# Storing every slot in pairs, with 32 KB pieces, in a streaming residual kernel

## The chip, the cores and the metric

The kernel runs on one core of a Trainium2 chip. The metric is the device time of one execution in microseconds; lower is better. The time before is 323.47 us, the median of three runs (323.29 to 323.54).

## The reference

For each of 128 samples a subject's number picks one of eight 128 x 128 weight matrices, and the sample is replaced by itself plus its product with that matrix, all in float32:

```python
w = weights[subjects]                          # (128, 128, 128) from (8, 128, 128)
out = jnp.einsum('bct,bcd->bdt', x, w)         # x is (128, 128, 1024)
return x + out
```

A sample is 128 x 1024 float32 values, 512 KB. 64 MB are read and 64 MB are written.

## The kernel before

A *slot* is four samples (`H * G` = 2 x 2), 2 MB: each of the 128 partitions holds 16 KB of it. SBUF holds 12 slots side by side in `x_all`, and the 32 slots of the input (`NT` = 32) pass through them in turn.

**Loads** are issued by ACT on its DMA queue, one DMA of 512 KB for each sample (`load`, line 127), with the source in rows of 16 KB. From slot 12 on, ACT waits until the slot's earlier content has been stored (line 205).

**GpSimd** waits for a slot's loads and releases TensorE through `s_ready` (lines 209 to 214). Loads and stores of a slot count on one semaphore, `s_slot`, so the counts are worked out by `emptied`.

**TensorE and VectorE** run a loop over the slots, in halves of two samples. `multiply` (line 159) does four matmuls into PSUM; `add` (line 174) adds the product to the slot in place and raises `s_added`, twice for each slot; `place` (line 154) copies the next weights.

**Stores** are issued by SP on its own DMA queue (line 216). Before a store SP waits for `s_added`: slot i is stored when slot i + 4 is added (`BEHIND` = 4), and the last eight slots (`LAST` = 8) without this delay. The first 20 slots are stored one at a time; the last 12 in pairs (`PAIR` = 2), each pair one DMA of 4 MB whose source is written as two pieces of 16 KB for each partition (`o=n`). The last pair's store stands behind the loop (line 240). Line 62, in the helper `transfer`, is the line of all these DMAs in the profile.

The order of DMAs in each of the two queues is that of the loops; both queues are worked on by the same 16 DMA engines.

Of the kernel before, what the change touches and what calls it, by code (L numbers as in the profile page):

```python
# [30 lines left out]
G = 2  # L31
H = 2
# [3 lines left out]
SLOTS = 12  # L36

P_SLOTS = 2

BEHIND = 4  # L40
LAST = 8

PAIR = 2

DMA = 16

# [8 lines left out]
def transfer(nc, engine, out, in_):  # L55

    later, nc._always_lower_symbolic_ap = nc._always_lower_symbolic_ap, False
    ins, outs = engine.lower_ap_dma(in_), engine.lower_ap_dma(out)  # L60
    nc._always_lower_symbolic_ap = later
    return engine.add_instruction(
        mybir.InstDMACopy(
            name=nc.get_next_instruction_name(),
            engine=engine.engine,
            ins=ins,
            outs=outs,
            mode="Copy",
            cce_op=ALU.bypass,
            queue=QUEUES[engine.engine],  # L70
        )
    )


@with_exitstack
def kernel(
    ctx: ExitStack,
    tc: tile.TileContext,
    x: bass.AP,
    subjects: bass.AP,  # L80
    weights: bass.AP,
    out: bass.AP,
):
    nc = tc.nc
    B, C, T = x.shape
    S, _, D = weights.shape
    NT = B // (G * H)

    def sbuf(name, *shape, dtype=F32):
        return ctx.enter_context(nc.sbuf_tensor(name, list(shape), dtype)).ap()  # L90


    room = -(nc.sbuf_base + -nc.sbuf_base % 32) % ALIGN
    if room:
        sbuf("room", C, room // 4)
    x_all = sbuf("x_all", C, SLOTS * H * G * T)
    xs = [
        x_all[:, i * H * G * T : (i + 1) * H * G * T].rearrange("c (q t) -> c q t", t=T)
        for i in range(SLOTS)
    ]  # L100
    w_all = sbuf("w_all", C, S, D)
    ws = [sbuf(f"w{i}", C, 1, D) for i in range(H * G)]
    zeros = sbuf("zeros", C, N)
    given, near, wrap = (sbuf(name, 1, B, dtype=I32) for name in ("given", "near", "wrap"))
    index = sbuf("index", 1, B + H * G, dtype=I32)
    ps = [
        ctx.enter_context(nc.psum_tensor(f"ps{i}", [D, G, T], F32)).ap() for i in range(P_SLOTS)
    ]

    s_given = tc.alloc_semaphore("s_given")  # L110
    s_wall = tc.alloc_semaphore("s_wall")
    s_index = tc.alloc_semaphore("s_index")
    s_zeros = tc.alloc_semaphore("s_zeros")
    s_product = tc.alloc_semaphore("s_product")
    s_added = tc.alloc_semaphore("s_added")

    s_ready = tc.alloc_semaphore("s_ready")
    s_go = tc.alloc_semaphore("s_go")

    s_slot = [tc.alloc_semaphore(f"s_slot{k}") for k in range(SLOTS)]  # L120
    s_head = tc.alloc_semaphore("s_head")

    def emptied(i):
        turns = i // SLOTS
        return DMA * (H * G + 1) * turns - (DMA * G if i >= SLOTS and i % SLOTS == 0 else 0)

    def load(engine, i, q):
        transfer(
            nc,
            engine,  # L130
            xs[i % SLOTS][:, q, :],
            x[i * H * G + q].rearrange("(a r) t -> a (r t)", r=ROWS),
        ).then_inc(s_head if i * H * G + q < G else s_slot[i % SLOTS], DMA)

    def store(i, n):
        at = i % SLOTS * H * G * T
        return transfer(
            nc,
            nc.sync,
            out[i * H * G : (i + n) * H * G].rearrange("g d t -> d g t"),  # L140
            x_all[:, at : at + n * H * G * T].rearrange("d (o t) -> d o t", o=n),
        )

    def subjects_of(i):
        _, subject = nc.values_load_multi_w_load_instructions(
            index[0:1, i] if isinstance(i, slice) else index[0:1, bass.ds(i * (H * G), H * G)],
            engines=[mybir.EngineType.DVE],
            min_val=0,
            max_val=S - 1,
            skip_runtime_bounds_check_because="the index is clamped on the chip above",  # L150
        )
        return subject

    def place(h, subject):
        for q in range(h * G, (h + 1) * G):
            copy = nc.vector.tensor_copy(ws[q], w_all[:, bass.ds(subject[q], 1), :])  # L156
        copy.then_inc(s_go, 1)

    def multiply(slot, h):
        nc.tensor.wait_ge(s_go, 1).then_inc(s_go, -1)  # L160
        nc.tensor.wait_ge(s_ready, 1).then_inc(s_ready, -1)  # L161
        for q in range(h * G, (h + 1) * G):
            for t in range(0, T, N):
                at = slot * (H * G * T) + (q * T + t)
                mm = nc.tensor.matmul(  # L165
                    ps[h][:, q % G, t : t + N],
                    ws[q][:, 0, :],
                    x_all[:, bass.ds(at, N)],
                    start=True,
                    stop=True,  # L170
                )
        mm.then_inc(s_product, 1)

    def add(slot, h):
        mine = x_all[:, bass.ds(slot * (H * G * T) + h * G * T, G * T)]
        nc.vector.wait_ge(s_product, 1).then_inc(s_product, -1)  # L176
        nc.vector.tensor_tensor(  # L177
            mine, ps[h].rearrange("d g t -> d (g t)"), mine, ALU.add
        ).then_inc(s_added, 1)

    with tc.tile_critical():  # L181

        nc.sync.dma_start(given, subjects.rearrange("(o b) -> o b", o=1)).then_inc(s_given, DMA)
        nc.sync.dma_start(w_all, weights.rearrange("s c d -> c s d")).then_inc(s_wall, DMA)

        nc.vector.memset(zeros, 0.0).then_inc(s_zeros, 1)  # L186
        nc.tensor.wait_ge(s_zeros, 1)
        for _ in range(IDLE):
            nc.tensor.matmul(  # L189
                ps[P_SLOTS - 1][:, G - 1, :N], zeros[:, :D], zeros, start=True, stop=True  # L190
            )

        nc.vector.memset(index[:, B:], 0).then_inc(s_index, 1)  # L196
        nc.vector.wait_ge(s_given, DMA)
        nc.vector.tensor_scalar(near, given, -S, S - 1, ALU.max, ALU.min).then_inc(s_index, 1)  # L198
        nc.vector.wait_ge(s_index, 2)
        nc.vector.tensor_scalar(wrap, near, 0, S, ALU.is_lt, ALU.mult).then_inc(s_index, 1)  # L200
        nc.vector.wait_ge(s_index, 3)
        nc.vector.tensor_tensor(index[:, :B], near, wrap, ALU.add).then_inc(s_index, 1)  # L202
        for i in range(NT):
            if i >= SLOTS:
                nc.scalar.wait_ge(s_slot[i % SLOTS], emptied(i))
            for q in range(H * G):
                load(nc.scalar, i, q)

        for i in range(NT):
            if i == 0:  # L210
                nc.gpsimd.wait_ge(s_head, DMA * G).then_inc(s_ready, 1)
                nc.gpsimd.wait_ge(s_slot[0], DMA * G).then_inc(s_ready, 1)
            else:
                nc.gpsimd.wait_ge(s_slot[i % SLOTS], emptied(i) + DMA * H * G).then_inc(s_ready, H)

        for i in [*range(NT - SLOTS), *range(NT - SLOTS, NT, PAIR)]:
            n = 1 if i < NT - SLOTS else PAIR
            nc.sync.wait_ge(s_added, (i + n + (BEHIND if i < NT - LAST else 0)) * H)
            if i + n < NT:
                store(i, n).then_inc(s_slot[i % SLOTS], DMA)  # L220


        nc.vector.wait_ge(s_index, 4)
        nc.vector.wait_ge(s_wall, DMA)
        subject = subjects_of(slice(0, H * G))
        for h in range(H):
            place(h, subject)
        with nc.vector.Fori(0, NT) as turn:  # L228
            subject = subjects_of(turn + 1)
            for h in range(H):  # L230
                add(turn % SLOTS, h)
                place(h, subject)
        with nc.tensor.Fori(0, NT) as turn:
            for h in range(H):
                multiply(turn % SLOTS, h)

    with tc.tile_critical() as waits:
        for i in range(NT - SLOTS, NT - PAIR, PAIR):
            nc.scalar.wait_ge(s_slot[i % SLOTS], emptied(i + SLOTS))
    last = store(NT - PAIR, PAIR)  # L240

    tc.add_manual_dep(
        last.ins,
        waits.name,
        mybir.DependencyInfo(mybir.DependencyClass.NoSync, mybir.DependencyReason.SCHED_ONLY),
        reason="the end of the program waits for it",
    )
# [27 lines left out]
```

## Time and profile before

| What | Value |
|---|---|
| Median of 3 runs | 323.47 us |
| The profiled execution | 323.24 us |
| Its span | 321.5 us |
| TensorE busy (matmuls) | 249.8 us, 78% |
| VectorE busy | 165.7 us, 52% |
| Bytes moved by the DMA engines | 134.76 MB, 419 GB/s over the span |
| Mean granted TensorE clock | 0.905 |

The span is the profiled stretch; the execution's own time is 1.74 us longer. In the rows of DMA queues, q10 is ACT's queue (the loads) and q1 is SP's (the stores, the weights and the subjects' numbers); after the name stand the packets, the megabytes, and the time that the packets took as a share of the 16 engines' time in the window. A row of a timeline has the start and the duration in us, then engine, line, operation, operands and count, and in brackets the engine's idle time just before, with what ended it. The rows of digits show a span or window in 40 equal slices, each digit the busy share in tenths.

### The profile page before, as it was taken

The numbers are of one execution on the slowest core, as the hardware profiler recorded it, in microseconds if no ns is written. First come the engines' busy times: TensorE is split into PE (matmuls) and PEld (weight loads), VectorE is DVE, ScalarE is ACT, GpSimd is POOL, SyncE is SP. The second block draws the span as 40 slices with busy tenths as digits, with TensorE's granted clock in tenths as the row PEclk, the third lists the DMA queues.
The fourth block names the chain that finished last, engine by engine and source line by source line (L and its number), as shares of the span: only waits on it lengthen the run. The fifth ranks groups of instructions, "written<-read, shape, count | busy, mean of one in ns | idle before, by whom it ended". The sixth has DMA issues, their size and how long they took to land. (4 is left out here: it accounts for less than half of the span.)

```text
span 321.5 us, 2368 instructions
## 1 busy us (share of the span) xinstructions
PE 249.8 (78%) x518; PEld 102.8 (32%) x518; DVE 165.7 (52%) x202; POOL 0.2 (0%) x4
## 2 busy tenths in 40 slices
PE   6999999999979666866888469999769995885000
PEld 2444444444433322322333124433323332331000
DVE  2377667767773366146365361776445766066000
POOL 0000000000000000000000000000000000000000
PEclk9999999999997799779999896999978999599555
DMA  7999999999999999999999999999999999999997
GB/s 283 428 424 424 426 424 391 428 426 426 428 432 428 423 430 424 426 424 424 426 426 428 430 430 426 426 426 428 424 424 424 420 426 430 426 428 424 430 424 318
DMA packets 11700, 134.76 MB, mean 419 GB/s; under 512 B 2482, under 2 KB 3507, under 8 KB 3507
## 3 DMA queue, kind: packets, MB, share of 16 engines
q10 hardware_dynamic: 6144, 67.12, 49.7%
q1 hardware_dynamic: 5554, 67.64, 49.7%
q14 instruction: 2, 0.01, 0.0%
HBM read 67.63 MB, written 67.11 MB: 419 GB/s over the span
## 5 line engine op out<-in xcount | busy, mean ns | idle before, releaser
L165 PE MATMUL ps<-x_all,w 128*128 x512 | 244.4, 635 | 42.2 <-PEq L161 27.6
L177 DVE TENSOR_TENSOR x_all<-ps,x_all 128x2048 f32 x64 | 146.6, 2291 | 124.9 <-DVEq L176 124.9
L165 PEld LDWEIGHTS ps<-x_all,w 128*128 128x128 f32 x512 | 101.0, 203 | 186.3 <-issue 185.8
L156 DVE COPY w<-w_all 128x128 f32 x132 | 23.1, 218 | 4.1 <-DMA w_all<-in_L_cond_weights_dram 4.1
L189 PE MATMUL ps<-zeros 128*128 128x512 f32 x6 | 5.5, 1088 | 1.7 <-DVE zeros L186 1.7
L189 PEld LDWEIGHTS ps<-zeros 128*128 128x128 f32 x6 | 1.8, 328 | 3.7 <-issue 2.1
L186 DVE MEMSET zeros<- 128x512 f32 x1 | 0.5, 485 | 1.0 <-SPq L181 1.0
L198 DVE TENSOR_SCALAR near<-given 1x128 int32<-1x128 int32 x1 | 0.2, 214 | 0.7 <-DMA given<-in_itok_B_dram 0.7
L202 DVE CUSTOM_DVE_ANT_0 index<-near,wrap 1x256 uint16<-1x256 uint16 x1 | 0.3, 280 | 0.0
L200 DVE TENSOR_SCALAR wrap<-near 1x128 int32<-1x128 int32 x1 | 0.2, 216 | 0.0
L262 POOL MEMSET const-bfloat16-1.0<- 128x1 bf16 x1 | 0.1, 101 | 0.0
L262 POOL MEMSET const-uint8-127<- 128x1 uint8 x1 | 0.1, 101 | 0.0
L262 POOL MEMSET const-float32-0.0<- 128x1 f32 x1 | 0.1, 98 | 0.2 <-issue 0.2
L262 POOL MEMSET const-float32-1.0<- 128x1 f32 x1 | 0.1, 98 | 0.0
L262 DVE BASE_LOAD x1 | 0.0, 21 | 0.1
L196 DVE MEMSET index<- 1x4 int32 x1 | 0.1, 62 | 0.0
## 6 DMA issues: line engine op xcount, KB each, us to landing
x_all<-in_x_dram ACTq DMA_DIRECT2D x128, 512.0 KB, 34.9
out_dram<-x_all SPq DMA_DIRECT2D x20, 2048.0 KB, 15.6
out_dram<-x_all SPq DMA_DIRECT2D x6, 4096.0 KB, 28.6
w_all<-in_L_cond_weights_dram SPq DMA_DIRECT2D x1, 512.0 KB, 5.0
given<-in_itok_B_dram SPq DMA_DIRECT2D x1, 0.5 KB
```

What stands on the lines that cost most here:

```text
L156: copy = nc.vector.tensor_copy(ws[q], w_all[:, bass.ds(subject[q], 1), :])
L165: mm = nc.tensor.matmul(ps[h][:, q % G, t : t + N], ws[q][:, 0, :], x_all[:, bass.ds(at, N)], start=True, stop=True,)
L177: nc.vector.tensor_tensor(mine, ps[h].rearrange("d g t -> d (g t)"), mine, ALU.add).then_inc(s_added, 1)
L186: nc.vector.memset(zeros, 0.0).then_inc(s_zeros, 1)
L189: nc.tensor.matmul(ps[P_SLOTS - 1][:, G - 1, :N], zeros[:, :D], zeros, start=True, stop=True)
L196: nc.vector.memset(index[:, B:], 0).then_inc(s_index, 1)
L198: nc.vector.tensor_scalar(near, given, -S, S - 1, ALU.max, ALU.min).then_inc(s_index, 1)
L200: nc.vector.tensor_scalar(wrap, near, 0, S, ALU.is_lt, ALU.mult).then_inc(s_index, 1)
L202: nc.vector.tensor_tensor(index[:, :B], near, wrap, ALU.add).then_inc(s_index, 1)
L262: nc = _bacc.Bacc("TRN2", target_bir_lowering=False, num_devices=1)
```

## The change

All 32 slots are stored in pairs. A pair's source is one piece of 32 KB for each partition (`o=1`); its destination is the same eight samples as for a pair before. SP issues the store of the pair (i, i + 1) when slot i + 4, the third behind the pair, is added (`BEHIND` = 3); the last eight slots wait for their own adds alone, as before. Stores have six semaphores of their own, `s_store`, one for each pair of slots in SBUF; ACT waits for one of them before it loads into the first slot of a pair, and `s_slot` counts loads alone. The compute on TensorE and VectorE is unchanged.

```diff
-BEHIND = 4
+PAIR = 2
+
+BEHIND = 3
 LAST = 8
-
-PAIR = 2
...
-    def emptied(i):
-        turns = i // SLOTS
-        return DMA * (H * G + 1) * turns - (DMA * G if i >= SLOTS and i % SLOTS == 0 else 0)
+    s_store = [tc.alloc_semaphore(f"s_store{k}") for k in range(SLOTS // PAIR)]
+
+    def stored(i):
+        return s_store[i % SLOTS // PAIR], DMA * (i // SLOTS + 1)
+
+    def loaded(i):
+        return s_slot[i % SLOTS], DMA * H * G * (i // SLOTS + 1) - (DMA * G if i % SLOTS == 0 else 0)
...
-    def store(i, n):
+    def store(i):
         at = i % SLOTS * H * G * T
         return transfer(
             nc,
             nc.sync,
-            out[i * H * G : (i + n) * H * G].rearrange("g d t -> d g t"),
-            x_all[:, at : at + n * H * G * T].rearrange("d (o t) -> d o t", o=n),
+            out[i * H * G : (i + PAIR) * H * G].rearrange("g d t -> d g t"),
+            x_all[:, at : at + PAIR * H * G * T].rearrange("d (o t) -> d o t", o=1),
         )
...
         for i in range(NT):
-            if i >= SLOTS:
-                nc.scalar.wait_ge(s_slot[i % SLOTS], emptied(i))
+            if i >= SLOTS and i % PAIR == 0:
+                nc.scalar.wait_ge(*stored(i - SLOTS))
             for q in range(H * G):
                 load(nc.scalar, i, q)
...
-        for i in [*range(NT - SLOTS), *range(NT - SLOTS, NT, PAIR)]:
-            n = 1 if i < NT - SLOTS else PAIR
-            nc.sync.wait_ge(s_added, (i + n + (BEHIND if i < NT - LAST else 0)) * H)
-            if i + n < NT:
-                store(i, n).then_inc(s_slot[i % SLOTS], DMA)
+        for i in range(0, NT, PAIR):
+            nc.sync.wait_ge(s_added, (i + PAIR + (BEHIND if i < NT - LAST else 0)) * H)
+            if i + PAIR < NT:
+                store(i).then_inc(stored(i)[0], DMA)
...
-    last = store(NT - PAIR, PAIR)
+    last = store(NT - PAIR)
```

6 lines of the change are left out of this document (3 added, 3 removed).

## The prediction

> **What bounds the kernel now.** I read the page first: the slices of the span, the DMA queues, the DMA issues.
>
> ```profile
> span 321.5 us, 2368 instructions
> DMA  7999999999999999999999999999999999999997
> q10 hardware_dynamic: 6144, 67.12, 49.7%
> q1 hardware_dynamic: 5554, 67.64, 49.7%
> out_dram<-x_all SPq DMA_DIRECT2D x20, 2048.0 KB, 15.6
> out_dram<-x_all SPq DMA_DIRECT2D x6, 4096.0 KB, 28.6
> ```
>
> The sixteen DMA engines are 90% busy or more in every slice but the first and the last, and the two queues fill 99.4% of them: ACT's loads (q10) and SP's stores (q1). So only two things move the time: the DMA engines' own work, and gaps in it. The packet counts tell the pieces. A load of 512 KB in pieces of 16 KB is 32 packets and 16 small ones that raise the semaphore; 128 x 48 = 6144. A 2 MB store is 128 + 16 and a 4 MB store 256 + 16; 20 x 144 + 6 x 272, with 1042 for the weights and the index, is 5554. So every piece is one packet of 16 KB now.
>
> Then the DMA view in three windows: late (stores alone), early (weights in pieces of 512 B), and with both queues full.
>
> ```profile
> DMA packets 493, 7.67 MB, mean 426 GB/s; under 512 B 25, under 2 KB 25, under 8 KB 25
> q1 hardware_dynamic: 1041, 0.52, 38.6%
> q1 hardware_dynamic: 662, 9.80, 57.7%
> q10 hardware_dynamic: 668, 7.28, 43.0%
> ```
>
> First line, 300 to 318 us: 468 large packets in 16 x 18 us of engine time are 615 ns each, and 426 GB/s makes a slot (2.097 MB) 4.92 us. Second, 1.5 to 6 us: 38.6% of 16 x 4.5 us over 1041 packets is 26.8 ns for 512 B. The last two, 60 to 100 us, matter most: the queues moved the same number of packets, 662 and 668, but not the same bytes. The engines take turns by packet, whatever its size, and a load's little semaphore packets use up turns too. An engine serves a slot's store in 8 turns and one small one; in those 9 turns the loads get 6 large packets and 3 small ones, three quarters of a slot, and it all takes 14 x 0.615 = 8.6 us.
>
> Last, the end: the DMA view from 285 to 286, from 286 to the end and from 319 to the end, and the timelines of PE, DVE and SP.
>
> ```profile
> q10 hardware_dynamic: 6, 0.00, 0.3%
> DMA packets 936, 14.29 MB, mean 402 GB/s; under 512 B 64, under 2 KB 64, under 8 KB 64
> q1 hardware_dynamic: 936, 14.29, 94.7%
> DMA  0699690600000000000000000000000000000000
> 274.85 10.14 PE L165 MATMUL ps<-x_all,w 128*128 x16 [5.21 <-PEq L161]
> 286.53 7.13 PE L165 MATMUL ps<-x_all,w 128*128 x16 [1.54 <-PEq L161]
> 285.23 2.29 DVE L177 TENSOR_TENSOR x_all<-ps,x_all 128x2048 f32 x1 [0.81 <-DVEq L176]
> 293.90 2.29 DVE L177 TENSOR_TENSOR x_all<-ps,x_all 128x2048 f32 x1 [0.81 <-DVEq L176]
> 256.99 40.38 SPq L62 DMA_DIRECT2D out_dram<-x_all  x5
> ```
>
> The first line holds the last packets of the loads, semaphores alone: the last slot lands within this microsecond, I take 285.7. From PE's start to its second add's end the last slot takes 296.19 - 286.53 = 9.66 us, the one before, with a PE that came out of 5.2 us of idling, 287.52 - 274.85 = 12.67. The last store is issued at the end of SP's row, 297.37 less its issue of about 0.6. At 286 the engines still hold 14.29 MB of stores, 10.10 of them not of the last pair: 23.7 us of work that covers the 10.8 us from there to the last store's issue, with 13 to spare. **This reserve is what lets the last slot's work cost nothing.** The last bytes leave at about 319.5, 2.0 us before the span ends.
>
> **The change part by part.** *Fewer packets.* 16 stores x 128 pieces of 32 KB replace 4096 of 16 KB: 128 fewer per engine. The straight line through 26.8 ns at 512 B and 615 ns at 16 KB has 7.8 ns per packet beside its bytes: 1.0 us less work, and 32 KB in 1.222 us. No row shows a 32 KB packet; I keep 2 us of gain and 1 us of loss as ends. Ten fewer DMAs' semaphores are ten small packets per engine, 0.1 us at most.
>
> *Waits.* ACT waits for stores 10 times instead of 20 and GpSimd's counts change; PE's and DVE's instructions stay. SP's wait now holds a pair until its third follower is added, i + 5 slots for the pair (i, i + 1), which is the count that let slot i go before; the first store starts when it did. Behind SP's wait stand only later stores. ACT gets two slots back at once. Does the load queue run dry in the middle? When a pair goes, loads up to slot i + 11 are out and about i + 6.2 are in (below), so some five slots of loads are queued, and a pair's store lets less than two through. Nothing for the middle: the queue of loads covers it.
>
> *Turns.* A pair's store is still 8 turns and a small one per engine, but each moves 32 KB. Against 6 loads' packets it takes 8 x 1.222 + 6 x 0.615 = 13.5 us, and in this time loads move three quarters of a slot, as they did during **one** slot's store. A pair now moves 2.7 times as much as the loads beside it, instead of 1.33 times for a slot. As the rate per pair (four slot moves) is 19.7 us, the store queue empties in every turn, and stores follow the adds as closely as the waits let them. The bytes are the same; the order of them is not: the reserve of stores at the end goes.
>
> *The end, step by step.* How far loads lead the adds:
>
> ```profile
> q10 hardware_dynamic: 520, 5.57, 45.5%
> q10 hardware_dynamic: 144, 1.57, 107.1%
> 46.40 0.66 SPq L62 DMA_DIRECT2D out_dram<-x_all  x1
> x_all<-in_x_dram ACTq DMA_DIRECT2D x7, 512.0 KB, 8.0
> DMA  0000009994000099940003899999999999998433
> ```
>
> From 257 to 286 us (first line) 5.57 MB of loads are left, 2.7 slots, when 28 slots are added: the lead is 1.3. It is the 12 us or so of a slot's compute at the mean pace of 9.85 us a slot, so I keep 1.2 for after. The second and third: a store issued at 46.40 has no packet until 50.4; with loads in front it takes 4 us to start. The last two (1.5 to 6 us): into idle engines the first packets run some 1.3 us after ACT's first issue at 0.9.
>
> When slot 26 is added (27 slots), stores up to 21 are done and 28.2 slots loaded; the pairs 22 and 24 go together, pair 26 one slot later. 3.8 slots of loads are left. In the 4 us to the start, 0.8 of them pass; during three pairs, 3 x 13.5 = 40.5 us, 2.25 more. Slot 29 lands some 18 us into them and is added 12 us on, so pair 28 stands behind them without a gap. The 0.75 slot that is left takes all its 13.5 us. So the last load lands as the last store but one ends, and nothing is left to cover the last slot's work.
>
> The sum, against the profiled execution: all but the last pair's bytes were out at 319.5 - 9.85 = 309.65, less 1.0 for the packets: 308.65. Then 0.8 from landing to PE's start, 11.2 of compute (between 9.66 and 12.67), 0.6 for SP's issue, 1.3 to the first packet, 9.85 for 4.19 MB, 2.0 to the end: 334.4 us of span. The gap is 13.9 us. The profiled execution took 323.24, 1.74 more than its span, and the median of the runs is 0.23 higher: 336.4. A lead that is 0.3 slot larger brings the last load 5 us earlier and the time to 331. I take 335. The ends of compute, start and packets reach from 333 to 341 for this case.
>
> **The rivals.** *A smaller gap.* If loads lead by two slots at the 27th add, 3.0 are left: 0.8 and 2.2 pass by the end of pair 26, two slots' moves before 308.65 and so near 299, and pair 28 alone (9.85 us) then covers part of the last slot. PE starts near 300.8, the last store's first packet comes at 314 in place of 308.65: 5.3 us of gap, 327.8. For it: two loads that land together are added one after the other; against it, the 1.3 measured. It reaches from 326 to 331.
>
> *The reserve holds: faster.* If at the last load's landing over 14 us of stores other than the last pair, some 6 MB, are still queued, no gap opens and the fewer packets stay as the whole effect: 323.47 - 1.1 = 322.4. That takes loads finishing 14 us before the stores' end, which means that an engine evens out bytes, not packets. The 9.80 MB against 7.28 at equal counts speak against it.
>
> *The change doesn't do what it says: no change.* If a piece of 32 KB is cut into packets of 16 KB or less, turns and packets stay as they are; pairs still give loads three quarters of a slot per slot stored, the reserve survives, and 323.4 results. For it: the trace has no packet above 16 KB. Against it: pairs were written as two pieces of 16 KB each, and the count of 272 shows one packet for each piece as the instruction names it. [...]
>
> **How the numbers follow.** Gap of some 14 us, 333 to 341 and down to 331 with the larger lead: 0.58. Smaller gap, 326 to 331: 0.24. Reserve holds: 0.10. Pieces cut: 0.08. The first two are slower, 0.82 in all; the third faster by 0.3%, 0.10; the fourth within 0.2% (0.65 us, about what a measurement of this kernel can tell from no change), 0.08. The range, 326 to 341, takes in the first two and leaves 0.18 out. Likeliest: 335.
>
> **What would show it.** Packets on the stores' queue: 16 x 144 + 1042 = 3346; 5394 or more would mean cut pieces. With both queues full, equal packet counts but over twice the bytes on q1; equal bytes there would sink the forecast. A last load's landing at 300 to 309 in place of 285.7, and then a hole of 5 to 15 us in the DMA row, with DVE's last add inside it and the last store's 9.85 us alone behind it. If the last add ends with stores other than the last pair still running, the forecast is wrong, and the time is near 322. If holes stand in the middle, the loads starve and my cover for the middle was wrong.

## The result, and the profile after

The changed kernel takes 341.7 us (median of 6 runs, 339.75 to 344.56), the kernel before 323.33 us on the same chip: a ratio of 1.0584, with a 95% interval of 1.0551 to 1.0616. The forecast was slower at 335 us, within 326 to 341. The direction came, and the mechanism in the main; the size is 6.7 us off and 0.7 us beyond the range. Times are medians of all runs, while the ratios go by means without the runs that are over 1.5% above the fastest of their kernel and, in the experiments, without the profiled one, so a ratio can differ a little from the quotient of two medians. The profiled execution took 341.22 us, 1.82 more than its span.

From the page of the changed kernel:

```profile
span 339.4 us, 2358 instructions
DMA  7999999999999999999999999999999999997047
GB/s 286 427 427 429 425 423 423 419 419 419 417 411 405 428 411 415 436 423 427 411 427 434 444 402 425 419 407 423 429 405 431 409 432 431 431 431 326 0 185 309
q10 hardware_dynamic: 6144, 67.12, 47.7%
q1 hardware_dynamic: 3346, 67.63, 47.1%
```

The row of DMA digits has a 0 in it, and the GB/s below it fall to 0: all 16 engines stand still near the end. The stores' queue has 3346 packets, the number that whole pieces of 32 KB give. The shares of both queues are 47.7% + 47.1% of 339.4, 321.7 us for each engine; before they were 319.6. So of 17.9 us of span, 2.1 are busier engines and 15.8 are engines without work.

The turns, in the DMA view from 275 to 285 us:

```profile
q1 hardware_dynamic: 108, 3.15, 73.7%
q10 hardware_dynamic: 105, 1.05, 24.9%
```

Nearly equal packets, three times the bytes on the stores' queue. 3.15 MB are 96 packets of 32 KB; 73.7% of 16 x 10 us over 96 is 1.228 us for one.

Then the end: the DMA view from 313.5 to 328 us, the view of windows, and the timelines of PE, DVE and SP:

```profile
DMA  2000000000000000000000000000000000000000
q1 hardware_dynamic: 6, 0.03, 0.5%
q10 hardware_dynamic: 1, 0.00, 0.0%
314.00:328.00 14.00, 9.36 (x16) 3.78 (x16) 5.12 (x6) 0.00 (x0) 0.82 0.00 0
314.47 9.36 PE L169 MATMUL ps<-x_all,w 128*128 x16 [8.43 <-PEq L165]
324.07 2.29 DVE L181 TENSOR_TENSOR x_all<-ps,x_all 128x2048 f32 x1 [0.81 <-DVEq L180]
289.16 38.32 SPq L62 DMA_DIRECT2D out_dram<-x_all  x2
```

The last load lands just before 313.9 us (one small packet of q10 is left in the window, and the digits stop after the first). From 314 to 328 us the DMA share, the last but one column, is 0.00, while PE and DVE do the last slot. Its second add ends at 326.36, SP issues the last store at 326.94 (the row's end, 327.48, less an issue of 0.54), and those 4.19 MB run alone. Before, 14.29 MB of stores stood behind the last load; now the last pair alone does.

How the loads ended, in the DMA view from 295, 300, 305 and 310 us (5, 5, 5 and 4 us long):

```profile
q10 hardware_dynamic: 43, 0.44, 21.0%
q10 hardware_dynamic: 35, 0.34, 16.5%
q10 hardware_dynamic: 15, 0.15, 7.0%
q10 hardware_dynamic: 5, 0.02, 1.0%
```

They don't stop, they fade. At 300 us 0.51 MB are left; at the 0.105 MB/us of 275 to 285 us that is 4.9 us of work, but it lasts almost 14. The engines don't end together: those that are done with their loads go on with stores alone (95.1% of the engines' time from 305 to 310 us), and the slot waits for the slowest engine (PE starts at 314.47 us, the last load lands just before 313.9). The trace doesn't name a packet's engine, but with the engines full 99% of the packets (the kernel before from 240 to 300 us, the changed one from 260 to 295 us) start within 4 ns of the end of an earlier packet, which is taken for the one before on the same engine. Followed in this way, the 16 engines end their last loads from about 295 to 312 us here, and from 283 to 285 us in the kernel before.

### The profile page after: what moved, and what is told of

Read it like the earlier page. It is cut to its first block, busy times and chain, and to the rows that moved or that the text cites. A ratio compares the mean times of both kernels' runs of the same rounds, so it can differ in the third digit from the quotient of the medians.

```text
span 339.4 us, 2358 instructions
## 1 busy us (share of the span) xinstructions
PE 254.1 (75%) x518; PEld 105.0 (31%) x518; DVE 165.7 (49%) x202; POOL 0.2 (0%) x4
## 2 busy tenths in 40 slices
DMA packets 9491, 134.76 MB, mean 397 GB/s; under 512 B 2321, under 2 KB 3346, under 8 KB 3346
## 3 DMA queue, kind: packets, MB, share of 16 engines
q10 hardware_dynamic: 6144, 67.12, 47.7%
q1 hardware_dynamic: 3346, 67.63, 47.1%
## 5 line engine op out<-in xcount | busy, mean ns | idle before, releaser
L169 PE MATMUL ps<-x_all,w 128*128 x512 | 249.6, 647 | 68.1 <-PEq L165 66.2
L169 PEld LDWEIGHTS ps<-x_all,w 128*128 128x128 f32 x512 | 103.3, 207 | 214.4 <-issue 213.7
L193 PE MATMUL ps<-zeros 128*128 128x512 f32 x6 | 4.5, 903 | 1.7 <-DVE zeros L190 1.7
```

Source lines behind the costliest of these rows:

```text
L169: mm = nc.tensor.matmul(ps[h][:, q % G, t : t + N], ws[q][:, 0, :], x_all[:, bass.ds(at, N)], start=True, stop=True,)
L193: nc.tensor.matmul(ps[P_SLOTS - 1][:, G - 1, :N], zeros[:, :D], zeros, start=True, stop=True)
```

## The experiments

Three readings stood against each other. *Turns*: a 32 KB packet gets one turn like a 16 KB packet, so stores outrun the loads and nothing is left to cover the last slot. *Waits*: pairing, the third follower and slots given back two at a time open the hole. *Long pieces*: packets above 16 KB move worse by themselves.

**Pieces of 16 KB, everything else as changed.**

```diff
-            x_all[:, at : at + PAIR * H * G * T].rearrange("d (o t) -> d o t", o=1),
+            x_all[:, at : at + PAIR * H * G * T].rearrange("d (o t) -> d o t", o=PAIR),
```

> All slots are still stored in pairs with the new waits and semaphores, but a pair's source is two pieces of 16 KB again. Turns: a store's turn is no longer than a load's, so stores don't outrun the loads; the last load lands near 295 us instead of 313.7, stores are still queued when the last add ends, the hole of some 15 us goes, and the time is 323 to 325 us. Waits (pairing, the third follower, slots given back two at a time open the hole): the hole stays and the time stays at 340 us or more. Slow pieces (32 KB pieces move slower by themselves): no hole either, 323 us.

Measured: 323.91 us, 1.0024 of before (1.0014 to 1.0034). Its page, and its DMA view from 296 us on:

```profile
span 322.7 us, 2358 instructions
DMA  7999999999999999999999999999999999999996
q1 hardware_dynamic: 662, 10.06, 88.6%
```

No load packet is left after 296 us, and 10.06 MB of stores still are: the reserve is back. The pairing, the waits and the semaphores cost 0.7 us; 17.7 of the 18.4 us need the long piece.

**Long pieces for the last 12 slots alone**, in the kernel before:

```diff
-            x_all[:, at : at + n * H * G * T].rearrange("d (o t) -> d o t", o=n),
+            x_all[:, at : at + n * H * G * T].rearrange("d (o t) -> d o t", o=1),
```

> The kernel before with one edit: its six pairs, the last 12 slots, are stored from one piece of 32 KB for each partition. The first 20 slots, all waits and all semaphores are those of before. Turns: only the order of transfers in the last 80 us decides whether the last slot is covered, so a hole before the last store comes back, 4 to 15 us long, and the time is 327 to 338 us. Waits: nothing of the new waits is there, 323.3 us. Slow pieces: 12 of 32 slots, so three eighths of the 18 us, about 330 us, but spread over the last third and without a hole.

Measured: 329.14 us (four runs, 328.42 to 334.28), 1.0183 (1.0154 to 1.0212). The page and the windows view:

```profile
span 326.6 us, 2368 instructions
DMA  7999999999999999999999999999999999999847
310.00:315.00 5.00, 1.06 (x3) 0.19 (x1) 3.06 (x6) 0.00 (x0) 0.85 0.00 0
```

A hole of at least 5 us, without one of the new waits; and with all of them, but pieces of 16 KB, there was none. As the cause of the hole *waits* is out. The order at the end makes the hole, but 12 slots of it make a third of the loss only.

**Late pairs held.** The pairs from slot 20 on, whose slots are not loaded again, wait for 27 adds at least (`HOLD` = 27), so the pairs 20, 22 and 24 go together; pieces of 32 KB stay.

```diff
-            nc.sync.wait_ge(s_added, (i + PAIR + (BEHIND if i < NT - LAST else 0)) * H)
+            nc.sync.wait_ge(s_added, (i + PAIR + BEHIND if i < NT - SLOTS else max(i + PAIR, HOLD)) * H)
```

> The changed kernel, 32 KB pieces and all, but the pairs from slot 20 on, whose slots are never loaded again, are held until 27 slots are added. Turns: loads run alone for longer before these stores begin, the last load lands before 290 us, four pairs or more stand queued at the last add, no hole, and the time is 322.4 to 325 us, with what the long pieces themselves cost or save as the rest. Waits: more holding is no cure, 341 us or more. Slow pieces: the 18 us stay, without a hole.

Measured: 329.05 us, 1.0156 (1.0117 to 1.0195). The hole is gone, as turns have it; 4 us more are left than the upper end that I gave. **The same with pieces of 16 KB** (`o=PAIR`):

> The kernel with the late pairs held until 27 slots are added, which took 329.0 us without a hole, with pieces of 16 KB instead of 32 KB. If the 5.8 us that were left there are the price of long pieces in the stretch where loads and stores share the engines (engines that stall and end apart from each other), they go and the time is 323 to 324 us. If the hold cost them, the time stays at 328 us or more.

In this run and in the one with pieces of 4 KB, the load of the subjects' numbers (0.5 KB, at the start) was split as well, into two and eight pieces.

Measured: 324.12 us, 1.0022 (1.0012 to 1.0031). So the long pieces have a second price of some 5 us that is no hole before the last store. The pages of both, 32 KB first:

```profile
span 328.7 us, 2358 instructions
GB/s 283 433 425 421 435 423 421 407 433 423 429 397 435 389 422 399 425 429 427 429 405 423 435 421 435 419 405 423 397 427 429 429 409 437 439 427 419 439 427 80
span 323.0 us, 2358 instructions
GB/s 282 424 426 422 424 424 390 434 428 426 422 428 424 427 430 430 422 422 426 426 426 420 432 422 424 424 420 430 422 428 424 424 424 430 432 424 426 424 428 264
```

With 32 KB the rate dips below 410 GB/s again and again in the middle, and the last slice, where engines end apart, moves 80 GB/s. The DMA view of the run with 32 KB from 320 us to its end:

```profile
DMA  3997073090033700330300300000300000000000
q1 hardware_dynamic: 45, 0.95, 25.7%
```

At 426 GB/s 0.95 MB are 2.2 us of work, but packets still start near 326 us. So the better part of the second price in this kernel is engines that end apart.

**Where the second price arises.** Long pieces for the first 20 slots alone, and, in the held kernel, for the held pairs alone:

```diff
-            x_all[:, at : at + PAIR * H * G * T].rearrange("d (o t) -> d o t", o=1),
+            x_all[:, at : at + PAIR * H * G * T].rearrange("d (o t) -> d o t", o=PAIR if i >= NT - SLOTS else 1),
...
+            x_all[:, at : at + PAIR * H * G * T].rearrange("d (o t) -> d o t", o=1 if i >= NT - SLOTS else PAIR),
```

> The changed kernel with 32 KB pieces for the first 20 slots alone; the last six pairs are stored in pieces of 16 KB. Turns: near the end loads and stores share as before, so there is no hole, or one under 3 us. What is left is the price of long pieces in the stretch where the store queue empties and fills again and again (held pairs in 32 KB pieces took 329.0 us, in 16 KB pieces 324.1): 325 to 329 us, with engines that end apart. If the order at the end were all, and long pieces in the middle cost nothing: 323.5 to 324.2 us.

> The held kernel (late pairs wait until 27 slots are added) with 16 KB pieces for the first 20 slots and 32 KB pieces for the held pairs, whose queue doesn't empty between them. If the price of long pieces comes with the emptying and refilling of the store queue: 323 to 324.5 us, no hole. If it comes with any 32 KB packets beside loads: 326 us or more.

Measured: 327.37 us (four runs, 326.91 to 330.72), 1.016 (1.0104 to 1.0217), and 324.02 us, 1.0025 (1.0015 to 1.0034). So the price comes with the first 20 slots, where the stores' queue empties and fills again (in the changed kernel three times, for some 17 us each). Held pairs, whose queue stays full, cost nothing that shows; but only 309 of their 768 long packets ran beside loads, against 1280 for the first 20 slots. A price for every such packet would make 0.8 to 1.0 us there, and the kernel stood as near to the one before as its like with pieces of 16 KB. This favours the emptying and doesn't prove it.

The trace of the changed kernel tells a little more. From 60 to 260 us, half of the loads' packets take 616 ns or less, as before, but 98 of 2496 take over 700 ns, against 11 of 2530 before. Of these 98, 55 ran at 124 to 128 and at 244 to 248 us, where stores begin again after some 17 us of loads alone. Why they take longer, no run tells.

The losses don't add: 4.1 us for the middle, 5.9 for the end, 18.4 for both. With long pieces at the end alone, the engines' last loads end within 2 us of each other, in the changed kernel within some 18; so engines that the middle has driven apart seem to make the uncovered end longer. No run tests this by itself.

**Loads in pieces of 8 KB, stores in pieces of 16 KB:** the ratio of sizes is two again, with nothing above 16 KB (`ROWS = 2`, `o=PAIR`).

> All pairs in pieces of 16 KB, which by itself took 323.9 us without a hole, and loads in pieces of 8 KB: a store's packet is twice a load's again, with nothing above 16 KB. A pair's 17 turns let 0.85 slot of loads through, against 0.75 in the changed kernel and 1.4 with loads of 16 KB. Turns (only the ratio of sizes counts): the last load lands after 303 us, the hole comes back with 5 to 16 us, and the time is 329 to 342 us, some 3 us of it for more packets. Long pieces (what is above 16 KB does the harm): no hole, 324 to 327 us.

Measured: 331.65 us, 1.0269 (1.0227 to 1.031). The DMA view from 280 to 290 us, and the digits from 303.2 us to the end:

```profile
q1 hardware_dynamic: 202, 3.05, 71.7%
q10 hardware_dynamic: 194, 1.26, 30.1%
DMA  9999999999720000000000999999999999999000
```

Nearly equal packets, unequal bytes, and a hole of about 6.5 us (ten zeros of 0.65). So a ratio of two was enough for a hole. It makes 8.3 us of loss here, though, not 18.4: followed as above, the engines' last loads end within 4 us of each other (298.5 to 302.5 us), although the stores' queue stands empty for 16 to 18 us three times here too.

**The other way: stores in pieces of 4 KB** (`o=PAIR * H * G`).

> The changed kernel with eight pieces of 4 KB for each partition: a store's packet is a quarter of a load's. Turns: loads outrun the stores as far as the slots let them, the last load lands before 285 us, more than 30 us of stores are queued behind it, no hole. Packets: 768 more for each engine than with 16 KB; at 4 ns beside the bytes (32 KB packets took 1228 ns, twice 616 less 4) that is 3 us, about 327 us; at the 7.8 ns of my line 6 us, about 330 us. A last load after 300 us would speak against turns.

Measured: 324.68 us, 1.0043 (1.0026 to 1.006). The DMA view from 270 us on has no loads:

```profile
q1 hardware_dynamic: 5290, 21.28, 98.0%
```

The last load is in before 270 us, with 21.28 MB of stores behind it: the end of the loads moves from 270 to 314 us with the store's piece from 4 to 32 KB. 98.0% of 16 x 52.7 us over 5194 packets of 4 KB is 159 ns, 5 more than a quarter of 616. The price was below both of my figures, as the time shows. On the page of this run the two queues' shares of the span add to 100.2% (51.1% and 49.1%), so the recorded times of packets overlap, and a part of these 5 ns is no time of its own.

**The last pair as two single slots.**

```diff
+            if i + PAIR == NT:
+                nc.sync.wait_ge(s_added, (i + 1) * H)
+                store(i, 1).then_inc(stored(i)[0], DMA)
...
+    last = store(NT - 1, 1)
```

> The changed kernel, but the last pair is stored as two single slots in pieces of 16 KB, slot 30 as soon as it is added. Turns: slot 30 is stored in the hole, 4.9 us are left behind the last add instead of 9.85, and the time falls by 4 to 5 us, to about 337 us; the last load still lands near 310 us. If the hole were not a wait for the last slot's add, the time would stay near 341.5 us.

(`store` takes the number of slots here.) Measured: 337.1 us, 1.0444 (1.0396 to 1.0493), 4.6 us less than the changed kernel. The DMA view from 305 us to the end:

```profile
DMA  4996995959989975610000000000000889988800
```

The hole is a wait for the last add: slot 30, stored ahead of that add, took these 4.6 us out of the time.

**Loads in pieces of 32 KB too** (`ROWS = 8`).

> The changed kernel with loads in pieces of 32 KB too (16 packets and 16 small ones for each load). Turns: during a pair's store the loads get 4 or 5 packets of 32 KB instead of 6 of 16 KB, 1.1 slots instead of 0.75, so the loads end earlier and the hole shrinks to 2 to 8 us: 325 to 333 us. A hole of 14 us or more would speak against turns. Waits: nothing that it blames has changed, 341 us. Slow pieces: twice as many of them, slower than 341 us.

Measured: 369.3 us, 1.1425 (1.1345 to 1.1505). A miss for turns and waits. The figure of long pieces came, but not from the stores' packets, which cost nothing that shows in a full queue (above): loads alone became slow, so the time is no test of turns. The hole before the last store shrank, to about 9 us (345 to 353.6 us), less than forecast but in the direction of turns. The DMA view from 20 to 45 us, no store running:

```profile
DMA packets 384, 6.29 MB, mean 252 GB/s; under 512 B 192, under 2 KB 192, under 8 KB 192
q10 hardware_dynamic: 384, 6.29, 103.3%
```

The same window of the kernel before:

```profile
DMA packets 988, 10.73 MB, mean 429 GB/s; under 512 B 333, under 2 KB 333, under 8 KB 333
```

No version beat the kernel before.

## Why the prediction failed in size

*What bounds it.* Right: engines full, and the reserve behind the last load as the cover. Where 10.06 MB stood behind it there was no hole, where the last pair stood alone there was one of 14 us.

*Turns.* Right in the sharing: 108 packets against 105; 8 x 1.228 + 6 x 0.616 is 13.5 us for a pair, as forecast. But the stores' queue doesn't empty "in every turn": the changed kernel's trace has three long stretches of loads alone, some 17 us each, from 110, 170 and 230 us.

*Waits, and the cover in the middle.* Right: no hole opened there, and the waits cost next to nothing (0.7 us with pieces of 16 KB). "Nothing for the middle" holds for the supply of loads, which it was about. The middle runs slower all the same. The DMA view from 60 to 260 us, of the changed kernel and then of the kernel before:

```profile
DMA packets 5230, 84.13 MB, mean 421 GB/s; under 512 B 1414, under 2 KB 1414, under 8 KB 1414
q1 hardware_dynamic: 1479, 43.22, 51.1%
q10 hardware_dynamic: 3750, 40.90, 49.5%
DMA packets 6792, 85.29 MB, mean 426 GB/s; under 512 B 1586, under 2 KB 1586, under 8 KB 1586
q1 hardware_dynamic: 2995, 43.83, 51.6%
q10 hardware_dynamic: 3796, 41.46, 49.1%
```

The engines are as busy as before and move 1.4% less: 2.7 us of 200. So packets take longer; that belongs to the next step.

*Fewer packets.* This is the first step that failed. Forecast 1.0 us less work, measured 2.1 more: a difference of 3.1 us, above the upper end of 1 us of loss. From 275 to 285 us a 32 KB packet took 4 ns less than two of 16 KB (1228 against 2 x 616), half of what my line gave. Over the whole run nothing of it is left: the stores' queue took 159.9 us per engine (47.1% of 339.4), before 159.8 (49.7% of 321.5). The loads, which I had left alone, took 2.1 us longer per engine (47.7% of 339.4 against 49.7% of 321.5): in the rows above a load's packet takes 630 ns on average, before 617.

*The end, step by step.* This is the second step that failed, and it failed twice. The lead of the loads was 1.2 slots in my walk. In the changed kernel 27 slots are added at 258.1 us, and the DMA view from there on has this left to load:

```profile
q10 hardware_dynamic: 502, 5.41, 15.8%
```

2.6 slots, so the lead was 2.4 (the loads had run alone from 230 to 248 us): by my own rule the case of the smaller gap, with 327.8 us. It didn't come, because the walk took the 16 engines as one. Evenly shared, the loads would have ended near 305 us (300 plus the 4.9 above); the slowest engine ended at 313.9. The two errors have opposite signs (some 3.7 us earlier, some 8.9 later), and the walk's "nothing is left" came true for a reason that it doesn't hold.

*The sum.* The long case summed to 334.4 us of span; measured 339.4. The last load landed 5.2 us later than the walk had it (313.9 against 308.65); the rest takes back 0.2. In the walk's own terms 3.1 of the 5.2 us are the work that *Fewer packets* had wrong (309.65 plus 2.1 is 311.8), and 2.1 are what the two errors of the end leave. Compute took 11.9 us (314.47 to 326.36) instead of 11.2; from the issue to the end 12.5 (326.94 to 339.4) instead of 13.2. The terms behind the last load were right to 0.7 us each; the term in front of them was not. Taking 335 rather than the 336.4 of the sum, for the sake of a larger lead, cost another 1.4.

*The rivals.* The reserve didn't hold, and pieces weren't cut: the stores' queue has 3346 packets, and one of 32 KB had one turn (108 against 105 in 10 us).

## What to carry to other kernels

Here two queues on the same DMA engines shared them by packets (108 against 105 in 10 us, with 3.15 and 1.05 MB), so the size of one queue's pieces set the order in which both queues' work was done, although the bytes stayed the same. In a kernel that the DMA engines bound, ask what is still queued when the last load lands, and whether it covers the last tile's compute; here a piece of 32 KB for the stores used that reserve up (14.29 MB behind the last load before, the last pair's 4.19 after). When an end is walked through by hand, the last load is that of the slowest engine, not of the mean one (here 313.9 us, against some 305).

## What the runs showed of the hardware that was not expected

- Loads of 512 KB in pieces of 32 KB, 16 packets for each DMA, moved 252 GB/s alone (192 large packets in 103.3% of 16 x 25 us, 2.15 us for each), where pieces of 16 KB moved 429. Why was not settled.
- The 16 engines, which work on both queues, ended far apart: the loads that were left at 300 us faded until 313.9, 14 us instead of 4.9, and the engines' last loads ended within some 18 us of each other (before: 2). This showed where the stores' queue held 32 KB pieces and emptied in the middle (with the late pairs held, as a last slice of 80 GB/s); the changed kernel's runs also differ by 4.8 us among themselves, those of the kernel before, beside them, by 0.5.
- The 0.7 to 0.8 us that stay with the pairs where there is no hole and no price of long pieces (pieces of 16 KB, held or not, and long pieces for the held pairs alone: 1.0022 to 1.0025) are without a cause.
